# A graph network on one core: the lone column group of layers 1 and 2 as a 2x2 block product by seven half-width products

## The chip, the cores and the metric

The kernel runs on one core of one Trainium2 chip. The metric is the device time of one execution in microseconds (us); lower is better. The engines named below are TensorE (PE, matmuls; PEld are its weight loads), VectorE (DVE), ScalarE (ACT), GpSimd (POOL) and SyncE (SP, which here issues DMAs). Each works through a queue of its own in order, and they meet at semaphores.

## The reference

A layer norm with ReLU, three layers of an edge convolution with mean aggregation, and one linear map over the concatenation of all layers, added to x. There are 2,500 nodes with 256 features and 80,000 edges, sorted by destination.

```python
def _edge_conv(x, src, dst, W, b):
    xi = x[dst]
    xj = x[src]
    m = jnp.concatenate([xi, xj - xi], axis=-1) @ W + b
    s = jax.ops.segment_sum(m, dst, num_segments=N)
    cnt = jax.ops.segment_sum(jnp.ones((dst.shape[0],), m.dtype), dst, num_segments=N)
    return s / jnp.maximum(cnt, 1.0)[:, None]
...
h = jnp.maximum(_layernorm(x, axis=-1), 0.0)
xs = [h]
for W, b in ((W0, b0), (W1, b1), (W2, b2)):
    h = jax.nn.relu(_edge_conv(h, src, dst, W, b))
    xs.append(h)
x = x + jnp.concatenate(xs, axis=-1) @ Wf + bf
```

Because the edges are linear in x[src], the sum over edges is a product with the matrix A of edge counts (source by destination): s = A^T (h Wb) + cnt * (h (Wt - Wb)), where Wt and Wb are the upper and lower half of W.

## The kernel before

**Tiles and groups.** The 2,500 nodes lie in 20 tiles of 128 rows (NT), and two tiles are a node pair q (Q = 10). The columns of A, the destinations, come in windows of 6 nodes and are cut into five groups: four of 504 columns and a last of 486 (line 408, `alone`). `hT` holds the features turned (256 features as 2 x 128 partitions, nodes as columns). z = h Wb is kept as two one-pass float32r parts, `zh` and `zl` = z - zh, so that two fast matmuls stand for one exact one.

**Layer 0** (lines 1119 to 1160) goes through the groups one after the other. While PE multiplies group g (`layer`, line 925: 20 tiles x 2 outputs x 2 parts), the counts of group g+1 are built into the tile `a` by comparisons on DVE, small matmuls, and copies on ACT. At the end of a group `finish` (line 903) fills one row of the next `a` from the degrees and writes `a` to DRAM as bfloat16 by four DMAs of POOL's queue (`a_dram`). Units called `own` add the term of the node itself, from three parts of hT that `split_own` (line 1082) makes, one half of the features at a time; for the last group the first half is made in `by_count` (line 915) at the end of the group before it, and its products stand behind three tiles of the last group.

**Layers 1 and 2** (lines 1424 to 1488) each have two stages.

1. The *node stage*, ten steps, one for each node pair: `Nodes.multiply` gives z and the share of the output for two tiles (12 matmuls of 512 columns into two PSUM banks); `parts` scales z on ACT (`tmp`), casts it to `zh` (ACT), subtracts to `zl` (DVE) and adds the output share to `acc` (DVE); `combine` makes four sums of z's quarter blocks on DVE; `sums` casts them to `sh` (ACT) and `sl` (DVE); `Split` (line 1030) prepares, two steps ahead, hT of a later pair as three parts (one ACT, two DVE operations). Beside it runs `Alone` (line 1333), the product for the lone group of 486 columns: its block of A is read back as bfloat16, cast to float32r on ACT (`make`, 128 x 1008), and multiplied two steps later (`LAG`), eight matmuls of 486 columns into two banks; `own` adds the node's own term in full float32.
2. The *pair stage*: groups (0, 1) and (2, 3) are taken together (`Pair`, line 1246). A 2x2 block product by seven products instead of eight: the blocks b11, b21, b22 are cast on ACT; the sums r1 and r2 are added in bfloat16 on DVE and cast on ACT; r3 and r4 are made on DVE. There are five chunks of four tiles for a pair, hence 35 steps for each pair, of four matmuls of 504 columns. `Stream` (line 1383) makes a block five steps before its product (`LEAD`), and `take` (line 1307) empties each product's PSUM bank after the last chunk.

Tile pools set waits too: `ready` has 7 blocks, `stage` 4 tiles for staged loads and splits, `ps_left` and `ps_right` four PSUM banks each. In the node stage the nodes' banks go round over six, and the lone group holds two of `ps_left`. In the pair stage the seven products take four banks of `ps_right` first, then `ps_left` (`any_bank`, line 1171).

**Order.** Operations issued through `PEo`, `DVEo`, `ACTo`, `SPo` and `POOLo` stay in program order on their engine, so the order of the lines in the loop at 1432 is each engine's order.

Of the kernel before, what the change touches and what calls it, by code (L numbers as in the profile page):

```python
# [313 lines left out]
def by_windows(ctx: ExitStack, tc: tile.TileContext, x, src, dst, Ws, bs, Wf, bf, out, missing):  # L314
# [94 lines left out]
    a_dram = [dram.tile([P, NT, GS], BF16, name=f"a_dram{g}") for g in range(NG)]  # L409
# [493 lines left out]
    def finish(g, a):  # L903
        c0, n = group_of(g)
        if n < GS:
            DVEo.memset(a[:, :, n:].bitcast(F32), 0.0)
        ACTo.copy(a[PAD:PAD + 1, NT - 1, :n], cnt[PAD:PAD + 1, c0:c0 + n])
        for t in range(0, NT, 5):
            POOLo.dma_start(a_dram[g][:, t:t + 5, :], a[:, t:t + 5, :].bitcast(F32))
# [209 lines left out]

    extra = chain(degrees(0), finish(0, a), later_loads(), degrees(1))  # L1120
    for g in range(NG):
# [13 lines left out]
        else:  # L1135
            second.close()
            raw_pools.append(ctx.enter_context(tc.tile_pool(name="raw", bufs=1, side="right")))
# [18 lines left out]
        if g + 1 < NG:  # L1156
            run(finish(g + 1, a1))
            a = a1
        extra = chain(() if g else forms_of_own(), degrees(g + 2) if g + 2 < WG else ())
    first_layer.close()  # L1160
# [7 lines left out]
    def bank():  # L1168
        return next_bank(0, 6)
# [4 lines left out]
    tmps = ctx.enter_context(tc.tile_pool(name="tmps", bufs=6))  # L1174
# [11 lines left out]

    def tmp():
        return tmps.tile([P, 512], F32, name="tmp")
# [18 lines left out]
    class Nodes:  # L1207
# [9 lines left out]
        def parts(self):  # L1217
            q = self.q
            self.zf = tmp()
# [13 lines left out]
        def combine(self):  # L1233
            self.raw = tmp()
            combine(self.raw.rearrange("p (s n) -> p s n", s=4), self.zf.rearrange("p (s n) -> p s n", s=4))
# [10 lines left out]
    class Pair:  # L1246

        def __init__(self, l, i):
            self.l, self.i = l, i
            self.one, self.two = (slice(c0, c0 + n) for c0, n in map(group_of, pairs[i]))  # L1250
            self.bank, self.r = {}, {}
# [23 lines left out]
        def own_sum(self, i):  # L1275
            one, two, r = self.one, self.two, self.r
            if i == 0:
                r["r1"] = tmp()[:, :GS]
                DVEo.tensor_add(r["r1"], hT[:, 0, one], hT[:, 0, two])
            elif i == 1:  # L1280
                r["r2"] = tmp()[:, :GS]
                DVEo.tensor_add(r["r2"], r["r1"], hT[:, 1, two])
            elif i == 2:
                r["r3"] = tmp()[:, :GS]
                DVEo.tensor_sub(r["r3"], hT[:, 0, one], r["r2"])
            elif i == 3:
                r["r4"] = tmp()[:, :GS]
                DVEo.tensor_add(r["r4"], r["r2"], hT[:, 1, one])

        def multiply(self, c, part, what, made):  # L1290
# [3 lines left out]
            if c == Q // 2 - 1:  # L1294
                if part[0] == "x":
                    w = ws[self.l][0][:, part[2], part[1] * P:(part[1] + 1) * P]
                else:
                    w = wsum[:, part[1], :]
                m = {"b11": hT[:, 0, self.one], "b21": hT[:, 1, self.one], "b22": hT[:, 1, self.two]}.get(what)
                PEo.matmul(to, w, self.r[what] if m is None else m, start=False, stop=False)  # L1300
# [6 lines left out]
        def take(self, what):  # L1307
            m, one, two = self.bank.pop(what), self.one, self.two
            if what == "b11":
                self.e1 = tmp()[:, :GS]  # L1310
                ACTo.copy(self.e1, m)
            elif what == "b21":
                DVEo.tensor_add(hT[:, 0, one], m, self.e1)
            elif what == "b22":
                self.f = tmp()[:, :GS]
                DVEo.tensor_sub(self.f, self.e1, m)
            elif what == "r1":
                self.e5 = tmp()[:, :GS]
                ACTo.copy(self.e5, m)
                DVEo.tensor_add(self.f, m, self.f)  # L1320
            elif what == "r2":
                self.v = tmp()[:, :GS]
                DVEo.tensor_add(self.v, m, self.e1)
                DVEo.tensor_add(hT[:, 0, two], m, self.f)
            elif what == "r3":
                DVEo.tensor_add(self.v, m, self.v)
                DVEo.tensor_add(hT[:, 1, two], self.v, self.e5)
                ACTo.activation(hT[:, :, two], hT[:, :, two], AF.Relu, scale=-1.0)
            else:
                DVEo.tensor_add(hT[:, 1, one], m, self.v)  # L1330
                ACTo.activation(hT[:, :, one], hT[:, :, one], AF.Relu)

    class Alone:

        def __init__(self, l, order):
            self.l, self.order = l, order
            self.c0, self.n = group_of(alone)
            self.to = [ps_left.tile([P, 512], F32, name="bank")[:, :self.n] for _ in range(DC)]
            self.blocks = {}

        def make(self, p):
            q = self.order[p]
            to = self.blocks[p] = block()
            ACTo.copy(to[:, :, :GS], loaded[p // 2][:, q % 2 * 2:q % 2 * 2 + 2, :])

        def multiply(self, p):
            block = self.blocks.pop(p)
            for i in range(2):
                t = 2 * self.order[p] + i
                for o in range(DC):  # L1350
                    for z in (zh, zl):
                        unit[0] = PEo.matmul(self.to[o], tile_of(z, t)[:, o * P:(o + 1) * P], block[:, i, :self.n],
                                             start=False, stop=False)

        def own(self, o, c):
            PEo.matmul(self.to[o], ws[self.l][0][:, c, o * P:(o + 1) * P],
                       hT[:, c, self.c0:self.c0 + self.n], start=(c == 0), stop=(c == DC - 1))

        def end(self):
            for o in range(DC):  # L1360
                self.own(o, 1)
            for o in range(DC):
                ACTo.activation(hT[:, o, self.c0:self.c0 + self.n], self.to[o], AF.Relu)

    loaded = {}

    def load_alone(k, order):
        c = order[2 * k] // 2
        st = stage.tile([P, 8 * GS], BF16, name="staged").rearrange("p (t n) -> p t n", n=GS)[:, :4, :]
        SPo.dma_start(st, a_dram[alone][:, 4 * c:4 * c + 4, :])  # L1370
        loaded[k] = st
# [11 lines left out]
    class Stream:  # L1383
# [21 lines left out]
        def run(self, tick):  # L1405
            for n, (m, p, c, part, what, made) in enumerate(self.steps):
                self.make(n + LEAD + 1)
# [7 lines left out]
    AHEAD_H = 2  # L1415
    PLAIN = (2, 7)
# [7 lines left out]
    for l in range(1, L):  # L1424
        order = orders[l]
        lone = Alone(l, order)
        if l == 1:
# [138 lines left out]
```

## Time and profile before

| | us |
|---|---|
| median of 3 runs (461.80 to 462.26) | 462.20 |
| the profiled execution | 461.73 |
| its span, first to last instruction | 459.8 |
| layer 1: first node product to first pair product | 190.41 to 238.76 |
| layer 2: the same | 315.10 to 363.57 |

The granted clock is 1.00 of full speed all along. The views used below are: the page (busy time by engine, the chain of work that ended last), windows (busy time of each engine between two times, in us from the span's start), the timeline (start, length, engine, operation, what it writes and reads, count, and in brackets the idle time before it and what ended it), and groups (line, engine, operation, tiles and shapes, count, busy us, mean ns of one, idle before). The rows carry one line number, L282, since a helper issues nearly all operations; they are told apart by engine, tile names and shapes. A PE row's length is that of a pipelined matmul; the distance between starts is its rate.

### The profile page before, as it was taken

Reading aid. Unit: us, or ns where it says so; the run is one execution under the profiler, and the core shown is the slowest. Engines: PE = TensorE matmul, PEld = TensorE weight load, DVE = VectorE, ACT = ScalarE, POOL = GpSimd, SP = SyncE. Lnnn points to the kernel's source line nnn. Section 1 sums busy time; section 2 is a strip of 40 time slices with the busy share of each in tenths; the row PEclk is TensorE's granted clock in tenths of the full one; section 3 lists DMA queues with packets and bytes.
Section 4 is the critical chain, followed back from the end, with each engine's and each line's share of the span. In section 5 each row is a group of like instructions: output and inputs, shape, how many; then the busy total and the mean of one; then the engine's idle time right before and its main releaser. Section 6 shows DMA issues by size and latency. Waiting matters only on the chain.

```text
span 459.8 us, 7427 instructions
## 1 busy us (share of the span) xinstructions
PE 452.0 (98%) x2729; PEld 356.6 (78%) x2729; DVE 373.7 (81%) x720; ACT 313.0 (68%) x575; POOL 41.6 (9%) x75
## 2 busy tenths in 40 slices
PE   8999999999999999999999999999999999999995
PEld 4888877677778778878878868877788787688685
DVE  7999979899888946199979859886999687569795
ACT  4879878694945434387779839756877897497540
POOL 4770006101001010000000000000000000000000
PEclk9999999999999999999999999999999999999999
DMA  8320088982908249211396522011114855220014
GB/s 273 103 59 13 1 171 133 204 172 42 185 1 168 60 95 189 92 45 45 95 362 235 188 92 91 0 45 46 45 50 138 332 181 180 90 91 0 1 63 165
DMA packets 21784, 52.20 MB, mean 114 GB/s; under 512 B 1915, under 2 KB 12110, under 8 KB 21742
## 3 DMA queue, kind: packets, MB, share of 16 engines
q1 hardware_dynamic: 14110, 33.31, 21.9%
q0 software_dynamic: 5856, 16.48, 18.6%
q10 hardware_dynamic: 1776, 1.89, 1.2%
q8 instruction: 22, 0.36, 0.3%
q14 instruction: 20, 0.16, 0.1%
HBM read 36.21 MB, written 15.62 MB: 113 GB/s over the span
## 4 chain that ended last, share of the span: by engine, by line
PE 96%; DVE 3%; issue 0%; DVEq 0%
PE bank L282 87%; PE pz L282 8%; PE turned L282 1%; DVE one_n L282 1%; DVE one_m L282 1%; DVE own_h L282 0%; DVE hT L282 0%; DVE pick L282 0%; DVE behind L282 0%; DVE deg L282 0%; DVE acc L282 0%; DVE idle L516 0%; DVE acc L431 0%; DVE away L282 0%; DVE deg_b L282 0%
## 5 line engine op out<-in xcount | busy, mean ns | idle before, releaser
L282 ACT CAST block<-staged 128x1008 fp32r<-128x1008 bf16 x120 | 118.0, 1032 | 16.5 <-DVE staged L282 6.5
L282 PE MATMUL bank<-block,zh 128*128 128x504 f32 (+1 forms) x200 | 83.8, 419 | 0.0
L282 PE MATMUL bank<-a,zh 128*128 128x504 f32 (+1 forms) x200 | 82.0, 410 | 0.0
L282 PE MATMUL bank<-a,zl 128*128 128x504 f32 (+1 forms) x200 | 77.8, 389 | 0.0
L282 PE MATMUL bank<-block,zl 128*128 128x504 f32 (+1 forms) x200 | 77.3, 387 | 0.0
L282 ACT CAST a<-bank 128x480 fp32r<-128x480 f32 (+1 forms) x105 | 54.3, 561 | 31.3 <-PE bank L282 31.1
L282 DVE TENSOR_TENSOR one_m<-iota_m,key_m 128x2048 bf16<-128x2048 bf16 (+2 forms) x55 | 64.0, 1164 | 9.4 <-PE bank L282 9.1
L282 PE MATMUL bank<-block,sh 128*128 128x504 f32 x160 | 68.9, 430 | 0.0
L282 PE MATMUL bank<-block,staged 128*128 128x512 f32 (+1 forms) x288 | 62.8, 369 | 0.0
L282 PE MATMUL bank<-block,sl 128*128 128x504 f32 x160 | 62.6, 391 | 0.0
L282 PEld LDWEIGHTS bank<-block,staged 128*128 128x128 f32 x288 | 49.4, 188 | 10.2 <-issue 0.7
L282 DVE TENSOR_TENSOR block<-staged 128x1008 fp32r<-128x1008 bf16 x40 | 46.9, 1204 | 5.2 <-PE bank L282 3.9
L282 PEld LDWEIGHTS bank<-block,zh 128*128 128x128 f32 x200 | 37.6, 188 | 10.9 <-issue 2.5
L282 PEld LDWEIGHTS bank<-block,zl 128*128 128x128 f32 x200 | 37.6, 188 | 10.7 <-issue 3.2
L282 PEld LDWEIGHTS bank<-a,zh 128*128 128x128 f32 x200 | 37.7, 188 | 6.6 <-ACT a L282 0.3
L282 PEld LDWEIGHTS bank<-a,zl 128*128 128x128 f32 x200 | 37.8, 189 | 6.2 <-issue 0.2
L282 DVE TENSOR_TENSOR one_n<-iota_n,key_n 128x640 bf16<-128x640 bf16 (+2 forms) x110 | 42.4, 427 | 0.0
L282 PEld LDWEIGHTS <-one_m 128*128 128x128 bf16 x834 | 30.3, 98 | 13.8 <-issue 7.3
L282 PE MATMUL pz<-wbf,hT 128*128 128x256 f32 x160 | 38.3, 385 | 0.0
L282 PEld LDWEIGHTS bank<-block,sh 128*128 128x128 f32 x160 | 30.1, 188 | 10.3 <-issue 3.5
L282 PEld LDWEIGHTS bank<-block,sl 128*128 128x128 f32 x160 | 30.1, 188 | 9.4 <-issue 3.7
L282 DVE TENSOR_TENSOR staged<-staged 128x1008 bf16<-128x1008 bf16 x40 | 27.1, 678 | 12.0 <-ACT block L282 11.6
(190 smaller groups left out, 633.6 us busy)
## 6 DMA issues: line engine op xcount, KB each, us to landing
staged<-a_dram SPq DMA_DIRECT2D x52, 504.0 KB, 4.4
a_dram<-a POOLq DMA_DIRECT2D x20, 630.0 KB, 9.9
acc<-in_x_dram POOLq DMA_DIRECT2D x3, 640.0 KB, 12.0
out_dram<-acc SPq DMA_DIRECT2D x5, 256.0 KB, 2.2
acc<-in_x_dram SPq DMA_DIRECT2D x2, 512.0 KB
wbf<-in_L_gnn_Wf_dram SPq DMA_DIRECT2D x3, 256.0 KB
acc<-in_x_dram ACTq DMA_DIRECT2D x1, 768.0 KB
wt<-in_L_gnn_W_dram SPq DMA_DIRECT2D x3, 256.0 KB
```

The source lines that it names most:

```text
L282: return self.tc.keep_in_program_order(call(*args, **kwargs))
```

## The change

The lone group's 486 columns are seen as two overlapping halves of H = 244 columns, and each pair of tiles as two rows of a 2x2 block, so that layers 1 and 2 multiply the group as they do the pairs: seven products of 244 columns in place of eight half-blocks (14 matmuls a node pair in place of 8 of 486 columns). The blocks b11, b21, b22 go to DRAM as float32 and come back ready for PE; r1, r2, r3 are computed once, in layer 0, kept as bfloat16 and cast on ACT in every layer; r4 is kept as float32. The group now holds four PSUM banks, so the nodes go round over four. `take` is shared with the pairs. The step order in the node stage is new: the sums of the step before come first, then the nodes, the lone product, the lone load, the lone cast, and the split last. The pair's first three casts come ahead of the last sums, and the lone group's last product and its results come behind the pair's first three products (`HOLD` = 3; its two relus follow at the pair's 13th step, `RELUS` = 12). In layer 0 three of the ten sets of sums (`KEPT` = 3) are made before the lone group begins, the others beside it. The tiles of `tmps` double in size, from 512 columns to 1024, and halve in number. `wsum` and the own sums are made at the layer's start.

```diff
@@ finish(g, a)
-        if n < GS:
-            DVEo.memset(a[:, :, n:].bitcast(F32), 0.0)
         ACTo.copy(a[PAD:PAD + 1, NT - 1, :n], cnt[PAD:PAD + 1, c0:c0 + n])
+        if g == alone:
+            halves = a.bitcast(F32).rearrange("p (q h) n -> p q h n", h=2)
+            for h in range(2):
+                ACTo.dma_start(lone_dram[:, :, h, :], halves[:, :, h, :H])
+            ACTo.dma_start(lone_dram[:, :, 2, :], halves[:, :, 1, SECOND])
+        else:
+            for t in range(0, NT, 5):
+                POOLo.dma_start(a_dram[g][:, t:t + 5, :], a[:, t:t + 5, :].bitcast(F32))
@@ by_count(g)
-        if g > 1:
+        if 1 < g < alone:
             split_own(g, 0)
@@ layer 0
+    def sums_of_alone(a):
...
+        for q in range(Q):
...
+            DVEo.tensor_add(r1, one[:, 0, :], two[:, 0, :])
+            DVEo.tensor_add(r2, r1, two[:, 1, :])
+            DVEo.tensor_sub(r3, one[:, 0, :], r2)
+            DVEo.tensor_add(r4, r2, one[:, 1, :])
+            SPo.dma_start(sums_dram[:, q, :], place)
+            yield
...
-            extra = chain(shares(), (None for _ in range(4)), first_forms())
+            extra = chain((None for _ in range(2)), shares(), (None for _ in range(2)), first_forms())
...
+            if g == alone and u % 2 and u > 2:
+                next(seven, None)
...
             run(finish(g + 1, a1))
+            if g + 1 == alone:
+                seven = sums_of_alone(a1)
+                for _ in range(KEPT):
+                    next(seven)
+                split_own(alone, 0)
@@ pools of layers 1 and 2
-    def bank():
-        return next_bank(0, 6)
+    def bank(n=4):
+        return next_bank(0, n)
-    tmps = ctx.enter_context(tc.tile_pool(name="tmps", bufs=6))
+    tmps = ctx.enter_context(tc.tile_pool(name="tmps", bufs=3))
@@ take(what), shared now
+            if what == "b11":
+                self.e1 = self.temp()
+                ACTo.copy(self.e1, m)
+            elif what == "b21":
+                DVEo.tensor_add(hT[:, 0, one], m, self.e1)
...
@@ class Alone(Sevens)
+            banks = [ps_left.tile([P, 512], F32, name="bank") for _ in range(4)]
+            self.bank = {what: banks[k // 2][:, k % 2 * 256:k % 2 * 256 + H] for k, (_, what) in enumerate(SEVEN)}
...
+        def load(self, p):
+            st = stage.tile([P, 4 * GS], F32R, name="staged")
...
+            SPo.dma_start(blocks.bitcast(F32), lone_dram[:, self.order[p], :, :])
+            SPo.dma_start(sums, sums_dram[:, self.order[p], :])
...
         def make(self, p):
+            blocks, sums = self.blocks[p]
+            to = block().rearrange("p c (k n) -> p (c k) n", k=2)[:, :3, :H]
+            ACTo.copy(to, sums[:, :3 * H].rearrange("p (k n) -> p k n", k=3))
...
         def multiply(self, p):
+            blocks = self.blocks.pop(p)
+            for k, (part, what) in enumerate(SEVEN):
+                for z in range(2):
+                    unit[0] = PEo.matmul(self.bank[what], part_of(part, z, self.order[p]), blocks[k], start=False,
+                                         stop=(p == Q - 1 and z == 1), skip_group_check=True)
...
         def end(self):
+            for _, what in SEVEN:
+                self.take(what)
@@ Stream
-                if what == "r2":
+                if what == "r2" and m:
                     next(bias, None)
...
             for n, (m, p, c, part, what, made) in enumerate(self.steps):
+                if n == HOLD:
+                    held()
                 self.make(n + LEAD + 1)
@@ layers 1 and 2 (new loop)
+        combine(wsum, ws[l][0].rearrange("p c (o n) -> p (c o) n", o=2))
+        for k in range(4):
+            lone.own_sum(k)
+        if l == 1:
+            split(order[2])
+        for i in range(Q + LAG - 1):
+            if i == Q:
+                stream.make(3)
+            if pending:
+                pending.pop(0).sums()
             if i < Q:
+                n = Nodes(l, order[i])
+                n.multiply(splits.pop(order[i]), coming[0])
                 n.parts()
                 n.combine()
                 pending.append(n)
+            if i < 2:
+                lone.own(3 * i, 3 + 4 * i)
             if i >= LAG:
                 lone.multiply(i - LAG)
+            if i < Q:
+                lone.load(i)
+            if i:
+                lone.make(i - 1)
+            if i + AHEAD_H < Q and order[i + AHEAD_H] not in splits:
+                split(order[i + AHEAD_H])
+            if i >= Q - AHEAD_H:
+                stream.load(i - Q + AHEAD_H + 1)
+
+        def held():
+            lone.multiply(Q - 1)
+            stream.load(4)
+            stream.make(5)
+            lone.end()
...
+            if n == RELUS:
+                lone.relus()
-            if n == 3:
-                combine(wsum, ws[l][0].rearrange("p c (o n) -> p (c o) n", o=2))
```

More of the change, by code (lines that the diff above doesn't have):

```diff
@@ L1218, in parts @@
             q = self.q
-            self.zf = tmp()
+            self.both = two_tmps()
+            self.zf, self.raw = (self.both[:, k:k + 4, :].rearrange("p k n -> p (k n)") for k in (0, 4))
             for i, t in enumerate(self.two):
@@ L1294, in multiply @@
             if c == Q // 2 - 1:
[L1295 to L1300, printed above, removed]
+                w, m = self.own_factors(part, what)
+                PEo.matmul(to, w, m, start=False, stop=False)
             for k, j in enumerate((2 * c, 2 * c + 1)):
@@ L1305, in multiply @@
                                          stop=(c == Q // 2 - 1 and k == 1 and z == 1))
[L1307 to L1331, printed above, removed]
@@ L1333, in by_windows @@
-    class Alone:
+    class Alone(Sevens):
         def __init__(self, l, order):
             self.l, self.order = l, order
-            self.c0, self.n = group_of(alone)
-            self.to = [ps_left.tile([P, 512], F32, name="bank")[:, :self.n] for _ in range(DC)]
-            self.blocks = {}
-        def make(self, p):
-            q = self.order[p]
-            to = self.blocks[p] = block()
-            ACTo.copy(to[:, :, :GS], loaded[p // 2][:, q % 2 * 2:q % 2 * 2 + 2, :])
-        def multiply(self, p):
[L1347 to L1357, printed above, removed]
-        def end(self):
[L1360 to L1371, printed above, removed]
+            c0, n = group_of(alone)
+            self.one, self.two = slice(c0, c0 + H), slice(c0 + n - H, c0 + n)
+            banks = [ps_left.tile([P, 512], F32, name="bank") for _ in range(4)]
+            self.bank = {what: banks[k // 2][:, k % 2 * 256:k % 2 * 256 + H] for k, (_, what) in enumerate(SEVEN)}
@@ new lines, in __init__, with temp @@
+            self.blocks, self.r, self.free, self.late = {}, {}, [], []
+        def temp(self):
+            if not self.free:
+                t = two_tmps()
+                self.free = [t[:, 2 * k:2 * k + 2, :].rearrange("p k n -> p (k n)")[:, :H] for k in range(4)]
+            return self.free.pop(0)
+        def load(self, p):
+            st = stage.tile([P, 4 * GS], F32R, name="staged")
+            blocks = st[:, :3 * H].rearrange("p (k n) -> p k n", k=3)
+            sums = st[:, 4 * H:7 * H].bitcast(BF16)[:, :5 * H]
+            SPo.dma_start(blocks.bitcast(F32), lone_dram[:, self.order[p], :, :])
+            SPo.dma_start(sums, sums_dram[:, self.order[p], :])
+            self.blocks[p] = [blocks[:, k, :] for k in range(3)], sums
@@ new lines, in make, with own @@
+        def make(self, p):
+            blocks, sums = self.blocks[p]
+            to = block().rearrange("p c (k n) -> p (c k) n", k=2)[:, :3, :H]
+            ACTo.copy(to, sums[:, :3 * H].rearrange("p (k n) -> p k n", k=3))
+            self.blocks[p] = blocks + [to[:, k, :] for k in range(3)] + four_sums(sums)[3:]
+        def own(self, i, j):
+            for k, (part, what) in list(enumerate(SEVEN))[i:j]:
+                PEo.matmul(self.bank[what], *self.own_factors(part, what), start=(k % 2 == 0), stop=False,
+                           skip_group_check=True)
@@ L1373, in steps_of, with relus @@
+        def relus(self):
+            for cols, sign in self.late:
+                Sevens.relu(self, cols, sign)
     def steps_of(l):
```

131 lines of the change are left out of this document (81 added, 50 removed).

## The prediction

> **What bounds the kernel now.** I read the page first, then the windows by stage, then the timeline of one step. The chain that ended last and the busy shares come from the page:
>
> ```profile
> PE 452.0 (98%) x2729; PEld 356.6 (78%) x2729; DVE 373.7 (81%) x720; ACT 313.0 (68%) x575; POOL 41.6 (9%) x75
> ...
> PE 96%; DVE 3%; issue 0%; DVEq 0%
> ```
>
> TensorE is the bound. But a share hides how little room the others have; the windows for layer 1's node stage and first pair show it (span; PE, PEld, DVE, ACT, POOL busy; clock; DMA share; GB/s):
>
> ```profile
> 200.00:245.00 45.00, 45.00 (x196) 36.19 (x195) 40.37 (x82) 34.72 (x55) 0.00 (x0) 1.00 0.46 156
> 245.00:283.00 38.00, 38.00 (x156) 29.01 (x155) 30.74 (x38) 28.06 (x31) 0.00 (x0) 1.00 0.45 147
> ```
>
> PE never idles, at full clock, and DVE is busy 40.4 of 45 us. One step of that stage on PE (start, length, operation):
>
> ```profile
> 199.50 0.97 PE L282 MATMUL bank<-hT,wt 128*128 128x486 f32 x2
> ...
> 202.09 2.96 PE L282 MATMUL bank<-block,staged 128*128 128x512 f32 x12
> 204.88 0.39 PE L282 MATMUL bank<-block,zh 128*128 128x486 f32 x1
> ...
> 206.65 2.97 PE L282 MATMUL bank<-block,staged 128*128 128x512 f32 x12
> ```
>
> Starts tell the rate: the node product takes 204.88 - 202.09 = 2.79 us, the lone group's eight matmuls 1.77 (0.22 each); together 4.56. The group's full-float32 term `own` costs (202.09 - 199.50) - 1.77 = 0.82.
>
> **The change, part by part.**
>
> *PE, half-width products.* Per layer, 80 matmuls of 486 columns become 140 of 244. No row shows a one-pass matmul of 244 columns; the nearest are 256 columns and, below, the 128-column transposes:
>
> ```profile
> 11.07 0.44 PE turned L282 x4
> ...
> 439.91 5.86 PE L282 MATMUL bank<-block,staged 128*128 128x256 f32 x48
> 445.61 1.89 PE L282 MATMUL bank<-wbf,hT 128*128 128x256 f32 x8
> ```
>
> That is 5.70/48 = 0.119 above and 0.44/4 = 0.11 below; I take 0.114. 80 x 0.2193 = 17.54 becomes 140 x 0.114 = 15.96: **-1.58**. `own`: 4 x 0.82 = 3.28 becomes 7 x 0.82 x 244/486 = 2.88: **-0.40**. So 1.98 us less PE work a layer, 3.96 in two; by the bounds 1.3 to 2.5 a layer. A PE step falls to 2.79 + 14 x 0.114 = 4.39.
>
> [...] In the 256-column rows the load of each matmul's weights hides behind the matmul before it, or 0.119 apart could not be. [...]
>
> *ACT and DVE, the step's loop.* The new order puts the cast of the sums `sh(i-1)` ahead of the two bank reads `tmp(i)`; before, it came after `zh(i)`. Rows of before for every link:
>
> ```profile
> 210.81 0.69 DVE L282 TENSOR_TENSOR zl<-tmp,zh 128x512 fp32r<-128x512 f32 x1 [0.18 <-ACT zh L282]
> 211.42 0.87 DVE L282 SCALAR_TENSOR_TENSOR acc<-bank,share,acc 128x256 f32<-128x256 f32 x2
> 212.21 1.06 DVE L282 TENSOR_TENSOR tmp<-tmp 128x256 f32<-128x256 f32 x3
> 213.19 0.68 DVE L282 TENSOR_TENSOR staged<-hT,staged 128x512 fp32r<-128x512 f32 x1
> ...
> 214.52 0.69 DVE L282 TENSOR_TENSOR sl<-tmp,sh 128x512 fp32r<-128x512 f32 x1
> 215.36 0.69 DVE L282 TENSOR_TENSOR zl<-tmp,zh 128x512 fp32r<-128x512 f32 x1 [0.15 <-ACT zh L282]
> ```
>
> ```profile
> 211.22 0.60 ACT L282 CAST sh<-tmp 128x512 fp32r<-128x512 f32 x1
> 211.73 1.03 ACT L282 CAST block<-staged 128x1008 fp32r<-128x1008 bf16 x1
> ...
> 214.70 0.62 ACT L282 CAST zh<-tmp 128x512 fp32r<-128x512 f32 x1
> ...
> 324.71 0.83 ACT L282 ACTIVATE tmp<-bank,share 128x256 f32<-128x256 f32 x2
> 325.57 0.62 ACT L282 CAST zh<-tmp 128x512 fp32r<-128x512 f32 x1
> ```
>
> The chain is now closed: `zl` to the end of the combination 0.61 + 0.79 + 1.06 = 2.46, hand-over 0.03, `sh` 0.51, two `tmp` 0.86, `zh` to the next `zl` 0.66: **4.52 us**, above PE's 4.39. So ACT and DVE fall 0.13 a step behind. The slack: `zl(i)` comes 4.16 after a step's start (206.65 to 210.81); split(i+2) ends 0.61 + 0.79 + 0.98 + 1.33 + 0.1 = 3.81 after it, and PE wants that at 8.78, so a lag of 0.81 is free. PE then waits 0.14 a step: by the ledger below in steps 7 to 9 of layer 1 (**0.42**), and in steps 4 to 9 of layer 2 (**0.81**), whose second node pair has a part on DVE and lags sooner. The two banks fewer for nodes cost nothing: the sums leave them at about 5.6, wanted at 8.8. Nor does the lone cast, which shrinks to 732 columns: 0.80 by a line through 512 (0.61) and 1008 (1.03).
>
> *The transition to the pairs.* Before, it had no PE wait. I kept a ledger of the queues (an instruction starts at the later of its queue and its inputs plus 0.03), and tried it on before:
>
> ```profile
> 232.99 0.62 ACT L282 CAST zh<-tmp 128x512 fp32r<-128x512 f32 x1 [1.50 <-DVE tmp L282]
> ...
> 236.14 0.62 ACT L282 CAST sh<-tmp 128x512 fp32r<-128x512 f32 x1 [1.07 <-DVE tmp L282]
> 236.67 1.96 ACT L282 CAST block<-staged 128x1008 fp32r<-128x1008 bf16 x2
> ```
>
> It gives 232.92, 236.06, 236.58 and no wait of PE, as the trace has it. New durations are from these groups (mean ns after the bar):
>
> ```profile
> L282 DVE TENSOR_TENSOR block<-staged 128x1008 fp32r<-128x1008 bf16 x40 | 46.9, 1204 | 5.2 <-PE bank L282 3.9
> L282 DVE TENSOR_TENSOR staged<-staged 128x1008 bf16<-128x1008 bf16 x40 | 27.1, 678 | 12.0 <-ACT block L282 11.6
> L282 DVE TENSOR_TENSOR tmp<-tmp 128x128 f32<-128x128 f32 x40 | 11.7, 292 | 1.4
> L282 DVE TENSOR_TENSOR tmp<-tmp 128x256 f32<-128x256 f32 x20 | 8.3, 414 | 0.0
> L282 ACT CAST zh<-pz 128x256 fp32r<-128x256 f32 x1 | 0.4, 405 | 0.0
> ```
>
> So 244 columns take 0.40 on either engine. For the new kernel, layer 1, in us after the first matmul of the last node step (ACT in its new order: `zh(9)`, lone cast 8, the pair's b11, b21, b22, `sh(9)`, lone cast 9, r1, r2, the next chunk's b11, then the group's first result):
>
> | event | ready | PE wants it | wait |
> |---|---|---|---|
> | `zh(9)` 4.97-5.59; lone cast 8 | 6.31 | 5.08 (7th matmul of pair 8) | **1.26** |
> | b11, b21, b22 | 7.25, 8.19, 9.13 | 7.25, 8.2, 9.1 | 0 |
> | `sh(9)` 9.65, `sl(9)`, lone cast 9 | 10.36 | 10.5 | 0 |
> | r1: DVE add 10.96, cast | 12.02 | 11.67 | **0.39** |
> | r2 cast 12.96, b11' 13.90, copy of lone b11 14.21, DVE add 14.65: frees the PSUM bank for r2 | 14.65 | 12.97 | **1.71** |
>
> The last is the new one: the seven products hold all four left banks, the pair's fifth product needs the first of them, and the copy that empties it stands on ACT behind three casts. Layer 2 has the same with 0.90 in the first row. Sum of waits: 0.42 + 1.26 + 0.39 + 1.71 = 3.78 and 0.81 + 0.90 + 0.39 + 1.71 = 3.81, so a layer nets about **+1.8**, both **+3.6**. The group's eight adds on DVE (8 x 0.4) lie beside pair matmuls, as `wsum` and the own sums do beside the first node products; without that cover they cost 3.2 and 2.6 a layer.
>
> *Last groups of layer 0.* The split of the lone group's own columns moves from four units before the group's start to behind the relus, the row copy and three DMA issues now on ACT, and three quads of sums on DVE:
>
> ```profile
> 165.60 0.61 ACT L282 ACTIVATE own_h<-hT 128x486 fp32r<-128x486 f32 x1
> ...
> 169.84 0.59 ACT L282 CAST a<-cnt 1x486 fp32r<-1x486 bf16 x1
> ```
>
> ```profile
> 0.82 0.40 ACTq L282 DMA_DIRECT2D dst_i<-in_dst_dram  x1
> ...
> 1.76 0.56 ACTq L282 DMA_DIRECT2D acc<-in_x_dram  x1
> ...
> 172.73 1.48 PE L282 MATMUL bank<-own_h,own_w 128*128 128x486 f32 x6
> ```
>
> ACT is free at 170.43; three issues of 0.40 to 0.56 end at 171.6 to 172.1, the high part at 172.2 to 172.7, the two DVE steps (0.7 each) at 173.6 to 174.1. The three quads (12 adds, about 4.5 us from 165.7) are done by then. PE wants the third part at about 172.7: **+1.2** (0.9 to 1.7; 0 if the issues cost nothing and the parts come one by one). The other seven quads, 10 us of DVE, lie beside 20 us in which DVE was mostly idle.
>
> **Sum.** Both layers +3.6 and layer 0 +1.2 give +4.8 on the profiled execution's 461.73: 466.5; the median of the three runs, 462.2, lies 0.47 above that execution, so **467.0** against it. The transfers (687 KB a step instead of 504 KB every second step) I cost at nothing, since DMA stands at 0.46 in that window.
>
> **Rivals.**
> - *The PE saving is kept.* If ACT and DVE stay ahead (links 6% shorter than the rows, as my ledger needs), the waits vanish and 3.96 comes off: 458.2 to 459.5 with layer 0's wait or without. For it: ACT is busy only 34.7 of 45 us. Against it: its order, not its load, makes the waits. It decides from a loop under 4.39 us and a bank freed before 12.97. Chance 0.19; between this and no change some waits remain (same, 0.08).
> - *Loads late:* a step's 687 KB must land in some 4.1 us; if 0.7 later each, casts slip and a layer loses 2 more: 471. Chance 0.06.
> - *Weight loads no longer hidden:* if load (bounded by the transposes' 0.11) and stream (0.11) came one after the other, 140 x 0.22 = 30.8 us stand against 17.54, 12.9 more a layer with `own`'s 0.40 off: about 489. Against it: at 256 columns they hide. Chance 0.02.
> - *Below 256 columns the one-pass rate is lost:* every such float32r row has 256 or more. At `own`'s rate (0.82 x 244/486 = 0.41) 140 take 57.4, 39 us more a layer: about 541. Chance 0.03.
>
> **How the numbers follow.** Forecast 0.62; with the slower rivals, slower by over 0.2% has 0.73, same 0.08, faster 0.19 (0.2% is about what a measurement here can tell from no change). The range 458.5 to 470.5 takes in the first rival but for its end, and leaves out late loads and the two rare ones.
>
> **What would show it.** Matmuls of 244 columns starting 0.114 apart; node steps of 4.5 rather than 4.39; PE waits on ACT's block late in step 9 (about 1), on a staged sum (0.4) and on DVE before the pair's fifth product (1.7), twice; a gap of about 1 at the lone group's `own` near 172.5. I am wrong if PE stays without waits there.

## The result, and the profile after

| | before | changed | fastest variant (below) |
|---|---|---|---|
| median, us | 462.11 | 476.31 | 460.49 |
| ratio to before, with its 95% interval | 1 | 1.0307 (1.0289 to 1.0325) | 0.9974 (0.9963 to 0.9984) |
| profiled execution / its span, us | 461.73 / 459.8 | 476.66 / 474.9 | 460.76 / 458.9 |
| first product of layer 1, us | 190.41 | 196.21 | 190.93 |
| layer 1, us | 124.69 | 130.75 | 124.42 |
| layer 2 and the end, us | 144.7 | 147.9 | 143.5 |

The change costs 14.2 us where 4.8 were forecast. One execution of the half-tiles kernel below (902.69 us) and one of before measured beside it (499.54 us) lie far above the others of their kernels and are left out of the ratios. The page of the changed kernel gives busy shares, the granted clock in 40 slices, and the chain that ended last:

```profile
PE 456.6 (96%) x2861; PEld 361.9 (76%) x2861; DVE 397.1 (84%) x783; ACT 308.4 (65%) x579; POOL 39.8 (8%) x71
...
PEclk9999999999999998999999999999999989999999
...
PE 69%; DVE 16%; ACT 10%; issue 2%; DMA 1%; ACTq 1%; POOL 0%; DVEq 0%
```

PE had 96% of the chain before; now DVE and ACT hold 26% of it. Two slices of the clock are below full, where before had none. The windows name the places (columns as before):

```profile
172.00:178.00 6.00, 2.95 (x29) 1.48 (x27) 1.61 (x5) 0.61 (x1) 0.00 (x0) 0.93 1.00 304
177.20:180.50 3.30, 3.30 (x10) 2.41 (x11) 2.43 (x8) 1.56 (x2) 0.00 (x0) 0.50 1.08 355
178.00:196.00 18.00, 18.00 (x77) 15.29 (x78) 17.09 (x42) 5.11 (x9) 0.00 (x0) 0.93 0.64 211
...
243.00:257.00 14.00, 11.01 (x61) 8.55 (x60) 10.64 (x22) 11.33 (x16) 0.00 (x0) 1.00 0.96 320
382.00:385.30 3.30, 3.30 (x9) 2.58 (x8) 3.04 (x8) 2.31 (x4) 0.00 (x0) 0.50 0.92 323
```

In layer 0's last group PE works 2.95 of 6 us and then runs at half clock; the trace's clock record has the half rate from 177.13 for 3.41 us, and again from 381.93 for 3.41 us, 1.7 us lost in each. DVE, forecast as mostly idle beside this group, is busy 17.09 of 18 us. In before it was busy 3.80 + 3.97 of the 18 us from 172:

```profile
172.00:178.00 6.00, 6.00 (x28) 5.13 (x28) 3.80 (x10) 2.21 (x4) 0.00 (x0) 1.00 1.03 211
178.00:190.00 12.00, 12.00 (x56) 10.21 (x56) 3.97 (x6) 2.88 (x5) 0.00 (x0) 1.00 0.40 83
```

With the forecast's 10 us on top hardly any of these 18 us is left. The waits themselves, from PE's timeline of the changed kernel:

```profile
175.67 0.49 PE L282 MATMUL bank<-own_h,own_w 128*128 128x486 f32 x1 [2.62 <-ACT own_h L282]
...
201.01 0.65 PE L282 MATMUL bank<-hT,wsum 128*128 128x244 f32 x2 [1.05 <-DVE wsum L282]
...
211.42 0.50 PE L282 MATMUL bank<-block,staged 128*128 128x512 f32 x1 [0.75 <-DVE staged L282]
...
244.00 0.38 PE L282 MATMUL bank<-staged,sl 128*128 128x244 f32 x1
245.80 0.38 PE L282 MATMUL bank<-block,sh 128*128 128x244 f32 x1 [1.43 <-ACT block L282]
246.02 0.27 PE L282 MATMUL bank<-block,sl 128*128 128x244 f32 x1
...
251.57 0.49 PE L282 MATMUL bank<-block,sh 128*128 128x504 f32 x1 [0.17 <-ACT block L282]
...
254.14 0.50 PE L282 MATMUL bank<-block,sh 128*128 128x504 f32 x1 [1.39 <-DVE hT L282]
```

The last three are the transition of layer 1 (layer 2 has 0.98, 0.15 and 1.38). The three rows around 245.80 show that a wait costs more than its length: starts 1.80 apart where 0.11 is the rate, of which 1.43 is listed, and the next start comes 0.22 later instead of 0.11. That is 0.37 more for this wait; by the same reckoning the other waits of the two transitions cost 0.26 to 0.39 more than their length. What stands behind the first two waits is on ACT's and DVE's timelines:

```profile
169.90 0.61 ACTq L282 DMA_DIRECT2D lone_dram<-a  x1
169.92 0.59 ACT L282 ACTIVATE hT<-bank 128x504 f32<-128x504 f32 x1
170.53 0.59 ACT L282 CAST a<-cnt 1x486 fp32r<-1x486 bf16 x1
171.15 3.81 ACTq L282 DMA_DIRECT2D lone_dram<-a  x2
175.01 0.61 ACT L282 ACTIVATE own_h<-hT 128x486 fp32r<-128x486 f32 x1 [3.89 <-issue]
```

```profile
196.66 0.40 DVE L282 TENSOR_TENSOR lone_r<-lone_r,a 128x244 fp32r<-128x244 bf16 x1
199.83 0.43 DVE L282 TENSOR_TENSOR wsum<-wt 128x256 f32<-128x256 f32 x1 [2.77 <-DMA sums_dram<-lone_r]
```

The first DMA issue holds ACT 0.61 us, the other two 3.81 together (0.57 and 3.21); `own_h` waits behind them. And DVE finishes the last of the ten sets at 197.06, after layer 1 has begun, then waits 2.77 us until that set has landed in DRAM: `wsum` and `tmps` take the memory that the sets' pool has given up.

### The profile page after: what moved, and what is told of

Its sections match the earlier page's. It is cut to its first block, busy times and chain, and to the rows that moved or that the text cites. A ratio compares the mean times of both kernels' runs of the same rounds, so it can differ in the third digit from the quotient of the medians.

```text
span 474.9 us, 7859 instructions
## 1 busy us (share of the span) xinstructions
PE 456.6 (96%) x2861; PEld 361.9 (76%) x2861; DVE 397.1 (84%) x783; ACT 308.4 (65%) x579; POOL 39.8 (8%) x71
## 4 chain that ended last, share of the span: by engine, by line
PE 69%; DVE 16%; ACT 10%; issue 2%; DMA 1%; ACTq 1%; POOL 0%; DVEq 0%
PE bank L282 60%; PE pz L282 8%; DVE tmp L282 4%; DVE acc L282 3%; ACT tmp L282 3%; DVE zl L282 3%; ACT zh L282 3%; ACT sh L282 2%; ACT block L282 2%; DVE one_m L282 1%; DVE lone_r L282 1%; PE turned L282 1%; DMA acc<-in_x_dram 1%; ACTq L282 1%; DVE own_h L282 1%
## 5 line engine op out<-in xcount | busy, mean ns | idle before, releaser
L282 ACT CAST block<-staged 128x1008 fp32r<-128x1008 bf16 (+1 forms) x120 | 113.4, 993 | 20.9 <-DVE staged L282 12.7
L282 PE MATMUL bank<-block,sh 128*128 128x504 f32 (+1 forms) x220 | 84.8, 394 | 5.5 <-DVE hT L282 2.8
L282 PE MATMUL bank<-block,sl 128*128 128x504 f32 (+1 forms) x220 | 77.9, 363 | 0.0
L282 PE MATMUL bank<-block,staged 128*128 128x512 f32 (+1 forms) x288 | 64.9, 373 | 1.0 <-DVE staged L282 1.0
L282 PEld LDWEIGHTS bank<-block,sh 128*128 128x128 f32 x220 | 41.6, 189 | 17.4 <-ACT block L282 3.9
L282 PE MATMUL bank<-block,zh 128*128 128x504 f32 x120 | 52.2, 435 | 0.0
L282 PEld LDWEIGHTS bank<-block,sl 128*128 128x128 f32 x220 | 41.8, 190 | 9.4 <-issue 3.7
L282 PE MATMUL bank<-block,zl 128*128 128x504 f32 x120 | 47.0, 391 | 0.0
L282 PE MATMUL bank<-one_n,one_m 128*128 128x60 bf16 x834 | 36.2, 195 | 0.2 <-DVE one_n L282 0.2
L282 ACT CAST sh<-tmp 128x512 fp32r<-128x512 f32 x20 | 12.4, 620 | 30.2 <-DVE tmp L282 30.2
```

Of the source, the lines that this page charges most:

```text
L282: return self.tc.keep_in_program_order(call(*args, **kwargs))
```

## The experiments

**Idle work in the waits.** Is the half clock a price of the waits, and does it count?

```diff
+                if g == alone and i == 0:
+                    spare = bank()
+                    for _ in range(11):
+                        PE.matmul(spare, zh[:, 0, :P], zh[:, 0, :512], start=True, stop=True)
...
+            if i == Q and l == 2:
+                lone.fill(8)
...
+                if n == 4 and self.l == 2:
+                    lone.fill(12)
```

> The changed kernel with idle matmuls put into three of PE's waits: 11 of 512 columns (0.233 us each, 2.56 in all) before the lone group's own term in layer 0, and in layer 2 alone 8 and 12 of 244 columns (0.114 each) before the last but one lone product and before the pair's fifth product. They write a PSUM place that nobody reads. Theory 1 (the granted clock falls to half for 3.41 us because PE idles): the waits stay where they are, both half-clock stretches go, and 2 x 1.7 = 3.4 us come off 476.3: 472.9, with layer 2's part alone 474.6 if the short fills do not suffice. Rival (the half-clock stretches have another cause, the transfers at that time for example): 476.3 or a little more, half-clock rows as before.

Measured: 482.3 us, ratio 1.0448 (1.0431 to 1.0466). A miss as a whole, but the two places answer separately. Windows and PE's timeline:

```profile
172.60:175.40 2.80, 2.80 (x16) 2.02 (x13) 0.00 (x1) 0.61 (x1) 0.00 (x0) 1.00 0.98 303
177.20:180.50 3.30, 3.30 (x17) 2.79 (x17) 2.83 (x7) 1.56 (x2) 0.00 (x0) 1.00 1.08 354
```

```profile
200.56 0.65 PE L282 MATMUL bank<-hT,wsum 128*128 128x244 f32 x2 [2.31 <-DMA staged<-lone_dram]
...
383.88 1.43 PE L282 MATMUL bank<-zh 128*128 128x244 f32 x5 [4.27 <-DVE hT L282]
```

In layer 0 the transfers are the same (DMA share 1.08) and the own term still begins at 175.42 (175.67 without the fill), yet the clock stays at 1.00 and layer 1 begins at 194.50 instead of 196.21: the half clock came from PE's idleness, not from the transfers, and cost its 1.7 us there. But the wait at `wsum` grew from 1.05 to 2.31, so that only 0.45 us arrived at the second node product: DVE's lateness stood right behind PE's. In layer 2 the fill itself had to wait 4.27 us for the PSUM bank it writes, until the lone group's results had been taken. Behind this longer wait the granted clock is 0.63 on average from 383.90 to 392.00, 3.0 us lost where a stretch of the changed kernel loses 1.7. So the total shows the edit's own wait, and whether the changed kernel's wait of 1.38 there brings the half clock is not answered by this run.

**The wait in layer 0: queue, or place of the split?** One run changes the queue of the three writes, another puts the split back to its old place.

```diff
-                ACTo.dma_start(lone_dram[:, :, h, :], halves[:, :, h, :H])
-            ACTo.dma_start(lone_dram[:, :, 2, :], halves[:, :, 1, SECOND])
+                POOLo.dma_start(lone_dram[:, :, h, :], halves[:, :, h, :H])
+            POOLo.dma_start(lone_dram[:, :, 2, :], halves[:, :, 1, SECOND])
```

> The changed kernel, with the three writes of the lone group's blocks issued on POOL's queue in place of ACT's; the split of the own columns stays behind the quads. Theory 1 (ACT stood 3.2 us in the third issue, and that made PE wait): the high part is done near 171.2, the third part near 172.6, PE's wait at the lone group's own term falls from 3.05 to under 0.3, the first half-clock stretch goes (1.7), and DVE starts layer 1 some 3 us sooner against PE, so that the waits there (1.05 and 0.98) shrink to 1 or less: 469 to 471.5. Rival (DVE's quads, or the transfers themselves, hold up the own term): the wait stays at 2 or more, 475 to 476.5.

```diff
-        if 1 < g < alone:
+        if g > 1:
             split_own(g, 0)
...
-                split_own(alone, 0)
```

> The changed kernel, with the lone group's first own split back ahead of the group's relus, issues and quads, where it was before the change; the three writes stay on ACT's queue. Theory 1 (the place of the split behind the blocked issue is the fault, not the quads as such): no wait at the own term's first half, no half clock there, 469 to 471.5 as with the other queue. Rival a (the blocked issue then delays the second split or the forms of the next layer): 472 to 475, with a wait on ACT later in the group. Rival b (the quads are too much for DVE anyway): layer 1 still starts with 2 us of waits on DVE, 472 to 473.

Measured: 471.8 us for both (1.0212, 1.0195 to 1.0229; and 1.0216, 1.0199 to 1.0234), a little above the expected 469 to 471.5. With the other queue the own term runs without a wait and without half clock, and layer 1 begins with the old wait doubled, where 1 us or less was expected (PE's timeline):

```profile
172.38 0.93 PE L282 MATMUL bank<-own_h,own_w 128*128 128x486 f32 x3
...
196.25 0.65 PE L282 MATMUL bank<-hT,wsum 128*128 128x244 f32 x2 [2.00 <-DVE wsum L282]
...
206.65 0.49 PE L282 MATMUL bank<-block,staged 128*128 128x512 f32 x1 [0.71 <-DVE staged L282]
```

With the split early ACT is blocked longer still, to no harm for the first half, but DVE is done 0.6 later, its last set takes longer to land (DVE waits 3.29 us for it, 2.52 with the other queue), and the wait at `wsum` is 3.28, with half clock behind it (0.50 in 198.40 to 201.70); ACT's timeline:

```profile
170.68 4.57 ACTq L282 DMA_DIRECT2D lone_dram<-a  x2
```

So the blocked issue ahead of the split made the 3.05 us in layer 0, not the quads. Both bring layer 1's start back to 190.5, a gain of 5.7, of which 1.2 or more is lost again at `wsum`. The half-tiles run below and all after it use POOL's queue; the next run does not.

**The loop of the node step.** Prediction: the sums cast ahead of the bank reads closes a chain of 4.52 us. In the changed kernel the steps are 4.53 long (PE's timeline):

```profile
225.25 3.12 PE L282 MATMUL bank<-block,staged 128*128 128x512 f32 x12
...
229.78 3.14 PE L282 MATMUL bank<-block,staged 128*128 128x512 f32 x12
```

First the order alone was put back:

```diff
-            if pending:
+            if i >= Q - 1:
                 pending.pop(0).sums()
...
                 pending.append(n)
+                if 0 < i < Q - 1:
+                    pending.pop(0).sums()
```

> The changed kernel, with the cast of a node pair's sums put behind the next pair's parts again in steps 1 to 8 (the last two steps keep the new order). Theory 1 (the loop of sums cast, bank reads, zh, zl, accumulations and combination makes the 4.53 us step): steps fall to PE's own 4.39, layer 1's late start is made up in part, and 0.9 + 0.8 come off: 474.6, to 473.5 if ACT then also reaches the last casts sooner. Rival (PE's own rate or the memory makes the 4.53): steps stay 4.53 and the time 476.3.

Measured: 474.95 us (1.0289, 1.0272 to 1.0306). Steps became longer, 4.68 us, not 4.39. ACT's timeline says why: the bank read of a step waits for the sums' low part of two steps before.

```profile
218.49 0.84 ACT L282 ACTIVATE tmp<-bank,share 128x256 f32<-128x256 f32 x2 [1.44 <-DVE sl L282]
```

The gain came from elsewhere: the transition's first wait fell to 0.61, and the waits on splits near 211 are gone. In this profile layer 0 loses more to the half clock (the page's clock digit for 177.1 to 189.0 is 7, at least 2.4 us lost, where a stretch of the changed kernel loses 1.7), PE comes to layer 1 0.7 us later, and layer 2 has no half clock (the mean clock of 0.993 makes 3.3 us lost in the whole span, which leaves no room for another 1.7); the release run below has the same order at a mean clock of 1.000, and no waits on splits there either, which speaks for the order. Then the tiles were given back their old size too, z and sums apart:

```diff
-    tmps = ctx.enter_context(tc.tile_pool(name="tmps", bufs=3))
+    tmps = ctx.enter_context(tc.tile_pool(name="tmps", bufs=6))
...
-            self.both = two_tmps()
-            self.zf, self.raw = (self.both[:, k:k + 4, :].rearrange("p k n -> p (k n)") for k in (0, 4))
+            self.four = one_tmp()
+            self.zf = self.four.rearrange("p k n -> p (k n)")
...
-            combine(self.both[:, 4:8, :], self.both[:, 0:4, :])
+            raw = one_tmp()
+            self.raw = raw.rearrange("p k n -> p (k n)")
+            combine(raw, self.four)
```

> The changed kernel with the writes on POOL's queue and the sums cast behind the next pair's parts in steps 1 to 8 (as the two runs before have them, one each), and with the tiles of the pool of temporaries at their old size again: six of 512 columns, the node pair's z and its four sums in two separate tiles. Theory 2 (behind the parts, the sums cast makes a loop of 4.68 us only because z and sums share one tile, so that a bank read waits for the sums' low part of two steps before): steps fall to PE's 4.39, the lag of layer 1's start is made up over the steps, the first transition wait shrinks as it did with the sums later, and 2.5 to 3.5 us come off the 471.8 of the run with the other queue: 468.3 to 469.3. Rival (another link holds the step at 4.5 or more): 471 to 472.5.

Measured: 467.5 us (466.5 to 469.5), ratio 1.0132 (1.0086 to 1.0178), below the 468.3 to 469.3 expected. Node products now start 4.38 us apart (PE's timeline, two of them):

```profile
212.09 2.96 PE L282 MATMUL bank<-block,staged 128*128 128x512 f32 x12
...
216.47 2.96 PE L282 MATMUL bank<-block,staged 128*128 128x512 f32 x12
```

The order and the tile are two ways to the same loss: cast early, the sums hold up the next bank read; cast late, with z and sums in one tile, they hold the tile that the bank read needs. The early order with small tiles was not run. Layer 2's first transition wait is gone with it, layer 1's fell from 1.43 to 0.26.

**Layer 1's start.** Three of the seven later sets were given to POOL (on the other-queue kernel, with the split early):

```diff
+            by = POOLo if q in (4, 6, 8) else DVEo
-            DVEo.tensor_add(r1, one[:, 0, :], two[:, 0, :])
+            by.tensor_add(r1, one[:, 0, :], two[:, 0, :])
...
```

> The changed kernel with the writes on POOL's queue, the first own split early, and three of the seven later sets of sums of the lone group computed on POOL in place of DVE. Theory 3 (DVE's ten sets end after layer 0's last product, and their last write must land before layer 1's first DVE work, wsum, can take over the memory): DVE is done some 4.4 us sooner, the wait at wsum's product (2.0 to 3.3) falls to 0.3 or less and the next (0.9) too: 468.5 to 469.5. Rival a (POOL slows DVE down, or is itself the last to finish): the wait stays above 1, 470.5 to 472. Rival b (the wait at layer 1's start comes from loads queued behind the sums' writes): unchanged, 471.8.

Measured: 471.6 us (1.0203, 1.0181 to 1.0225), the wait at `wsum` 1.98: rival a. DVE's adds took longer beside POOL's (DVE's timeline beside POOL's adds and without them, then POOL's), and later DVE waited 1.28 us for a set of POOL's:

```profile
175.40 0.76 DVE L282 TENSOR_TENSOR lone_r<-a,lone_r 128x244 bf16<-128x244 f32 x1
...
180.98 0.41 DVE L282 TENSOR_TENSOR lone_r<-a,lone_r 128x244 bf16<-128x244 f32 x1
```

```profile
175.05 0.83 POOL L282 TENSOR_TENSOR lone_r<-lone_r,a 128x244 fp32r<-128x244 bf16 x1
```

The last set was still finished at 192.5, as without POOL. So this run couldn't speak for or against theory 3. The next one kept all work on DVE and changed its order (on the half-tiles kernel):

```diff
-            DVEo.tensor_add(r1, one[:, 0, :], two[:, 0, :])
-            DVEo.tensor_add(r2, r1, two[:, 1, :])
...
+        for qs in (0, 1, 2), (3, 4), (5, 6), (7, 8), (9,):
...
+            for (r1, r2, r3, r4), o, t in zip(sums, one, two):
+                DVEo.tensor_add(r1, o[:, 0, :], t[:, 0, :])
+            for (r1, r2, r3, r4), o, t in zip(sums, one, two):
+                DVEo.tensor_add(r2, r1, t[:, 1, :])
...
```

> The half-tiles kernel, with the lone group's sums made for two or three pairs of tiles at a time, their adds alternating so that no add reads what the one just before it wrote, and all done by layer 0's ninth unit beside the lone group instead of its fifteenth. Nothing is left out and nothing moves to another engine. Theory 3 (DVE finishes the sums too late: the last write to DRAM must land before layer 1 can reuse the memory): the last write lands well before layer 0's end, the 2.0 at wsum's product and the half clock after it (1.7) go: 464 to 465. Rival (the forms and splits that the sums push back are late in their place, or DVE's work is too much however ordered): a wait of 1 to 2 on a split or form at layer 1's start, 466 to 467.5.

Measured: 464.4 us (1.0047, 1.0033 to 1.0060). DVE's timeline:

```profile
187.91 0.41 DVE L282 TENSOR_TENSOR lone_r<-lone_r,a 128x244 fp32r<-128x244 bf16 x1
...
190.89 0.42 DVE L282 TENSOR_TENSOR wsum<-wt 128x256 f32<-128x256 f32 x1
```

The sets end at 188.3, `wsum` follows the splits with no wait, and the first node step takes 3.83 us instead of 6.06. The half clock behind that wait is gone too; this profile has one in layer 2 instead (the page's clock digit for 370.7 to 382.3 is 8). Theory 3 holds: done in time, the sets cost PE no wait at layer 1's start, and it was their last write that was late. The run weaves the adds and also places the sets earlier; which of the two would do alone is not shown.

**The transition.** The first attempt moved the pair's first cast and the lone cast 8 ahead, the first result's copy ahead of r1, and the next chunk's three products ahead of r2, r3 and r4 (on the other-queue kernel):

```diff
-            if i == Q:
-                stream.make(3)
+            if i >= Q - 1:
+                stream.make((1, 3)[i - Q + 1])
...
+                if i == Q - 1:
+                    lone.make(i - 1)
                 n.parts()
...
-            stream.make(5)
-            lone.end()
+            lone.take("b11")
+            stream.make(4)
+            lone.take("b21")
+            lone.take("b22")
+            stream.make(10)
```

> The changed kernel with the writes on POOL's queue and another order at the end of the node stage: the pair's first cast ahead of the last sums but one, the lone cast 8 ahead of node pair 9's parts, the copy of the lone group's first result ahead of the pair's r1 cast, the next chunk's three casts and products ahead of r2, r3 and r4. Theory 4 (the transition's waits of 1.42 + 0.17 + 1.39 and 0.99 + 0.14 + 1.39 are an order on ACT that leaves it idle before the sums and late after, and a bank freed late): 4 to 5 of these 5.5 us go: 467 to 468. Rival (ACT's and DVE's whole work there is more than PE's, so the waits only move to the next blocks): under 2 us come off, 470 to 471.8.

Measured: 476.9 us (1.0322, 1.0302 to 1.0342), 5.1 above its base. The cast moved ahead was ahead of its own load (ACT's timeline), and later casts waited in their turn (PE's):

```profile
238.93 1.03 ACT L282 CAST block<-staged 128x1008 fp32r<-128x1008 bf16 x1 [2.81 <-DMA staged<-a_dram]
```

```profile
240.54 0.38 PE L282 MATMUL bank<-staged,sh 128*128 128x244 f32 x1 [1.16 <-ACT sh L282]
...
256.59 0.50 PE L282 MATMUL bank<-block,sh 128*128 128x504 f32 x1 [1.15 <-ACT block L282]
...
258.87 0.49 PE L282 MATMUL bank<-block,sh 128*128 128x504 f32 x1 [1.10 <-ACT block L282]
```

The profile also has two stretches of half clock in layer 1's transition: from 242.42 to 245.37 and from 259.44 on, products of 504 columns start 0.42 apart, against 0.23 between. The base has one, in layer 2 (its page's clock digit for 376.4 to 388.2 is 8). The second attempt kept that order of products but left the end of the node stage alone, put the group's second copy ahead of two casts, and kept `acc`'s bias off DVE at this point (on the half-tiles kernel):

```diff
+            lone.take("b11")
+            stream.make(4)
+            lone.take("b21")
+            lone.take("b22")
+            stream.make(5)
+            lone.copy()
+            stream.make(9)
+            lone.take("r1")
+            stream.make(10)
...
-                if what == "r2" and m:
+                if what == "r2" and m > 1:
```

> The half-tiles kernel with the lone group's first two PSUM banks emptied sooner (both ACT copies ahead of most of the pair's casts) and the next chunk's three casts and products ahead of r2, r3 and r4; the end of the node stage stays as it is. Theory 4 (the wait of 1.39 before the pair's fifth product, in either layer, is the bank that the copy frees late): it goes, 0.3 to 0.8 of waits on casts takes its place in each layer, 465.5 to 467. Rival (ACT and DVE have no room there, as in the transition run): waits of the same sum or more in other places, 467 to 470.

Measured: 464.9 us (1.0062, 1.0044 to 1.0080). The wait for the bank is gone in both layers; layer 2 has 0.46 at the pair's first cast and 0.26 later in its place, and layer 1's transition is down to (PE's timeline)

```profile
237.92 0.38 PE L282 MATMUL bank<-block,sh 128*128 128x244 f32 x1 [0.26 <-ACT block L282]
...
243.76 0.50 PE L282 MATMUL bank<-block,sh 128*128 128x504 f32 x1 [0.25 <-ACT block L282]
```

**Together.** The woven sums and this second edit on one kernel:

> Both of these edits together. If theories 3 and 4 hold, the gains add: 461.5 to 463, about level with the kernel before. If only theory 3 holds: 464 to 466. If neither: 467 or more.

Measured: 461.5 us, 0.9991 (0.9981 to 1.0001): both hold, and the kernel is level with before. Two small edits more, the first alone and then both:

```diff
-                n.parts()
+                n.parts((lambda: lone.make(Q - 2)) if l == 1 and i == Q - 1 else None)
...
+            if between:
+                between()
             ACTo.copy(pair_of(zh, q), both)
```

> The kernel of both edits, and in layer 1's last node step the lone cast 8 moved into the 0.83 us in which ACT waits for DVE between the bank read and zh. Theory 4 again, at its smallest: layer 1's wait of 0.26 at the last but one lone product goes, and the casts behind it come 0.7 sooner, so that the 0.25 before r1 may go too: 0.3 to 0.6 off 461.5, 460.9 to 461.2. Rival: zh later makes another wait of the same size, 461.5.

```diff
-            if i < Q:
-                lone.load(i)
...
                 split(order[i + AHEAD_H])
+            if i < Q:
+                lone.load(i)
```

> The same with the lone group's load issued behind the split in every step, so that it takes over the staged tile of the split that the node product has just used, not that of the lone product two steps before: its load can start some 3 us sooner in the step, and the pair's first chunk follows without it in the queue. If layer 2's wait of 0.63 on the pair's first cast is that late load, it goes, and with the edit before 460.3 to 460.8 result, below the kernel before by 0.2 to 0.3%. Rival (the first chunk still waits for its own tile, or another load becomes late): no gain over the run before, or up to 1 us lost.

Measured: 460.5 us, 0.9974 (0.9963 to 0.9984), and 461.0, 0.9981 (0.9970 to 0.9991). The moved cast took layer 1's wait of 0.26 away; the 0.25 before r1 stayed. Its profile also lacks layer 2's wait of 0.63, where this edit does nothing; with the load moved PE waits 0.65 there again, since the pair's first cast still waited 0.80 for its chunk. So the moved load did not do what it was for, part of the step from 461.5 to 460.5 is how the loads fell in, and the intervals of the three kernels overlap. The kernel with the cast alone is the fastest measured, 0.26% below before, with an interval clear of no change. Of the 4.2 us of PE work saved, 0.9 arrives in its span; where the rest goes was not taken apart. The page of this kernel:

```profile
PE 449.7 (98%) x2861; PEld 360.5 (79%) x2861; DVE 394.6 (86%) x783; ACT 309.8 (68%) x579; POOL 42.3 (9%) x74
...
PEclk9999999999999999999999999999999999999999
```

## Why the prediction was right in sign and wrong in size

| term, us | forecast | in the trace of the changed kernel |
|---|---|---|
| PE work saved, both layers | -3.96 | -4.2 (14 matmuls in 1.59, rate 0.1135, where 8 took 1.76; own term 2.9 for 3.3) |
| layer 0's last group | +1.2 | +5.1 (waits 3.05, half clock 1.7, restarts) |
| layer 1's first steps | 0 | +2.9 (waits 1.05 + 0.75 + 0.22, restarts) |
| node steps' loop, both | +1.23 | +1.65 (4.53 against 4.38, in 6 and 5 steps) |
| transitions, both | +6.36 | +7.3 (waits 5.50, restarts) |
| half clock in layer 2 | 0 | +1.7 |
| start of the span, before layer 0's first products | 0 | +0.7 (56.81 for 56.12; 56.2 to 56.8 in the other runs) |
| sum | +4.8 | +15.2 (span: +15.1) |

**Right.** The saving to 0.3 us, its rate, and the own terms; that 244 columns keep the one-pass rate and hide their weight loads (0.1135 apart, for 0.119 at 256 columns); that the new order's chain is longer than PE's step (4.52 forecast, 4.53 seen); the three transition waits, each in its place with its releaser (1.26, 0.39 and 1.71 forecast for layer 1, 1.43, 0.17 and 1.39 seen). The transfers of the node stage cost PE nothing in the changed kernel, as said; with the transition shortened a late load shows, 0.78 us on ACT in layer 2 with both edits. Of the rivals, the one of weight loads no longer hidden fell: 140 matmuls a layer start 0.1135 apart, where load and stream one after the other were put at 0.22. The rival of a lost one-pass rate fell with the same rate, and its price was misread: the row of 0.82 us holds two matmuls, so that 140 at that rate would take 28.8 us a layer and not 57.4, and the time would be about 484 and not 541. The transitions' listed waits, 5.50, are even below the forecast 6.36; the restarts, which the prediction did not price, make them 7.3.

**Wrong, first: the issues in layer 0.** "three issues of 0.40 to 0.56 end at 171.6 to 172.1" took small transfers for the price of the third of three issues that move 3.7 MB. The first two took 0.61 and 0.57, near the forecast, the third 3.21. The place and the waiter were right; the term was mis-sized, 1.2 for 3.05. The run with another queue took that wait away whole; in the run with three sets on POOL, which has the same queue, two of the three issues took 1.87 together. Why the third holds ACT so long stays open.

**Wrong, second: the cover of DVE's work.** "The other seven quads, 10 us of DVE, lie beside 20 us in which DVE was mostly idle" compared sums of busy time, and even these left little: 10 beside 7.77 of 18. In the order written the quads ended after the stage, and their write to DRAM had to land before the next layer's first DVE work could have the memory. This also took away the cover that `wsum` and the own sums were said to have ("2.6 a layer" without it). The same work in another order removed the wait.

**Wrong, third: the clock.** The prediction read 1.00 in before's windows and took it for a constant. In the changed kernel it came down twice, 1.7 us each, behind waits of 3.05 and 1.38; with layer 0's wait filled it did not come down there. This term was left out. Its size is a matter of the execution: with the same wait before the pair's fifth product of layer 2 (1.4 for 1.38) the run with the sums later has no half clock there, and loses at least 2.4 us to it in layer 0.

The forecast's loop was right in mechanism (4.52 for 4.53), but it named the order alone. The runs showed that with z and sums in one tile the other order is slower still (4.68); the doubled tiles were not weighed at all.

## What to carry to other kernels

Free time of an engine in a window is no cover until the added work is placed in its queue, last write and reuse of its memory included: here 10 us were laid beside a stage in which DVE was already busy 7.8 of 18, and held up the next one by 1 to 2. A DMA issue on an engine that others wait for must be priced from issues of its own size and number: here the first two of three equal ones took some 0.6 us each and the third 3.21. And a wait on TensorE should be priced above its length, with the restart (0.26 to 0.39 us more in these transitions), and with a chance of half clock behind it (here two stretches of 3.41 us, 1.7 lost in each).

## What the runs showed of the hardware

- The same wait of 2.00 us at `wsum` was followed by half clock in the half-tiles run (0.50 in 198.00 to 201.20) and by none in the other-queue run (1.00 in 196.30 to 199.70). In the changed kernel both stretches lasted 3.41 us, and 201.39 us of full clock lay between them. PE was not idle throughout before either: it was busy 1.00 of the 3.40 us before the first (173.70 to 177.10) and 1.88 of the 3.41 us before the second (378.52 to 381.93). How much idleness brings the half clock was not shown.
- Three executions of the half-tiles kernel took 466.49, 467.52 and 469.48 us at mean granted clocks of 0.998, 0.995 and 0.991.
- In the run with three sets on POOL, adds of 244 columns on DVE took 0.65 to 0.83 us while POOL was adding too (rows from 173.93 to 176.07), and 0.41 while it was not (180.09 to 181.31).
- On DVE, 244-column adds that read what the add before wrote started 0.44 to 0.45 apart, and those that did not 0.32 to 0.33 (rows of the half-tiles kernel with woven sums: 186.69, 187.13, 187.58 and 182.80, 183.12, 183.45, 183.77), which is what the weaving gained beside the order.
